# Windowed attention in a four-layer kernel: exponentials divided before they are transposed, global queries' products in column strips, global values spread by a 0/1 matrix

## The chip, the cores and the metric

The kernel runs on one core of one Trainium2 chip. A core has five engines that run side by side, each with its own queue of instructions that it takes strictly in order: TensorE (PE, matrix products and transposes; loading of the stationary operand is shown as PEld), VectorE (DVE), ScalarE (ACT), GpSimd (POOL) and SyncE (SP, which here only issues DMAs). They share the SBUF; TensorE writes its results to eight PSUM banks. The metric is the device time of one execution in microseconds (us).

## The reference

A block of four layers is computed for x of shape 16 x 512 x 256 (16 batches, 512 positions, 256 channels), all in float32. Each layer adds its output to x after a layer norm of x:

```python
x = x + attn_a(layernorm(x))   # stage "a"
x = x + ffn(layernorm(x))      # stage "f"
x = x + attn_b(layernorm(x))   # stage "b"
x = x + ffn(layernorm(x))      # stage "h", the same weights as "f"
```

The change lies in `attn_a` alone. With 16 heads of 16 channels, half a window of 32 and 4 global positions:

```python
q, k, v = proj(Wq, bq), proj(Wk, bk), proj(Wv, bv)
scores = einsum('bhsd,bhtd->bhst', q, k) * 0.25
mask = (abs(i - j) <= 32) | (i < 4) | (j < 4)
attn = softmax(where(mask, scores, -inf))
out = einsum('bhst,bhtd->bhsd', attn, v)
return out @ Wo.T + bo
```

So most queries see a window of 65 keys and the first 4 keys ("global keys"), and the first 4 queries ("global queries") see all 512 keys. `ffn` is a gated product of three 768-wide matrices; `attn_b` is a causal attention over all 512 keys whose denominators come from unrotated queries and keys.

## The kernel before

**What sets the order.** Stages are written as Python generators that yield an `Op` ahead of each piece of work: its engine, an estimated duration, what it needs, which buffers it takes and gives back. `Plan.run` (line 142) keeps all threads of all stages and batches, and again and again puts out the one that can start first by its estimates. On PE, among pieces that can start within 0.05 us, it prefers a lower rank, then one that keeps the same way of lying in the array (`ROWS`, `COLS`: strips of 32; `FULL`), then the thread with the least `progress` (line 137: batch number, plus the stage's `LEAD`, plus the share of the stage's PE time that is done). The order of every engine's queue is therefore fixed when the program is built, and comes from these estimates. Up to four batches are in flight, each in another stage. The planner's estimates (`us=...`, and `LEAD`, `SHARE` in lines 192 and 193) take no part in the computation.

**Stage "a", for one batch** (`window_attention`, line 551). PE makes the keys `kp`, the queries `q` and the values `va` (`values`, line 500). POOL makes masked copies of the 4 global keys and queries, `kg` and `qg`, and `xg`, the first 4 columns of the normalized input repeated 16 times (lines 603 to 614). DMAs on SP copy `va` into two shifted versions `vw`. For each of four tiles `t` of 128 positions, PE makes the scores `sa` of the window (line 663), and then:

- `softmax` (line 674): DVE adds the mask into `sc`, 128 partitions x 16 heads x 132 scores (L693). Each half of eight heads then passes DVE maximum (L706), POOL addition of the negated maximum (L708), ACT exponential (L715) and DVE sum (L717); at the end DVE inverts all 16 sums (L723).
- `turns` (line 763): PE transposes the exponentials in four groups of four 128 x 128 blocks (L772); DVE and ACT take turns at copying them out to `pt` (L777, L779).
- `weights` (line 785): POOL gathers the global keys' exponentials (`pq`, L796) and spreads the inverted sums over 256 channels (`rdca`, L804, shown as the helper's L541). PE transposes `pq` (L809) and both halves of `rdca` (L811) into one PSUM bank; DVE and ACT copy them out to `pgs` (L816, L818).
- The weighted sum: PE multiplies `pt` by `vw` in column strips (L842, four strips of 32 output partitions side by side), and adds the global keys' part from `vg` (L855). `finish` (line 866): DVE multiplies the result by the transposed inverted sums (L872) to give `yt`, and PE projects it (`project_out`, L488).

`global_values` (line 728) makes `vg`, the values of the 4 global keys laid out block-diagonally: PE multiplies `xg` by `wv` (L733, two products, each of which the profile lists as two matmul records, as it does for every float32 product but not for a transpose), and DVE masks it with `g_diag` (L742). `global_queries` (line 883) makes the first 4 queries' outputs over all keys: scores `gq` (L890), maximum, exponential `gp` (64 rows x 512, L905), transposes `tg` (L916), the product with `va` (`og`, L930: four products of 64 x 256, which hold every head's weights against every head's values), the masked and scaled `om` on DVE (L939), and a second product that adds up the rows (`yg`, L945). Its result replaces the first 4 columns of `yt` (L875).

There are two `sc` buffers, and one of most others (the dictionary at line 364). The queries and keys of the next batch can only be made when this batch's last `sa` is done (the slot "a").

Of the kernel before, what the change touches and what calls it, by code (L numbers as in the profile page):

```python
# [191 lines left out]
LEAD = {"a": 0.0, "f": 1.0, "b": 2.0, "h": 3.0}  # L192
# [4 lines left out]
def kernel(  # L197
# [55 lines left out]

    def load_const(ap, shape, name):
        t = const.tile(shape, F32, tag=name, name=name)
        nc.scalar.dma_start(t, ap)
        return t
# [14 lines left out]
    g_sel = cglob[:, D : D + NG]  # L272
# [75 lines left out]
    def values_bias():  # L348
# [3 lines left out]
        for kc in range(NC):  # L352
# [25 lines left out]
            "rdc": 1,  # L378
# [172 lines left out]
    def window_attention(b):  # L551
        me = f"a{b}"

        def go(thread, rank=0):
            plan.start(thread, "a", b, rank)
# [32 lines left out]
        yield from values("a", b, va, wv_sb, 0, "va")  # L588

        def copies():  # L590
# [9 lines left out]
            0, *(f"kp_{me}.{oc}" for oc in range(NC)), *(f"q_{me}.{oc}" for oc in range(NC)), us=2.2  # L600
# [12 lines left out]
        xg = work.tile([P, NC, H, NG], F32, tag="xg", name=f"xg_{b}")  # L613
        nc.gpsimd.tensor_copy(xg, xnt[me][:, :, 0:NG].unsqueeze(2).to_broadcast([P, NC, H, NG]))
# [29 lines left out]
        go(global_values(b, xg))  # L644
# [29 lines left out]
    def softmax(b, t, op, ps, sg):  # L674
# [5 lines left out]
        small = buf(op, "small", [P, 3, H], f"sm_{b}_{t}")  # L680
# [22 lines left out]
        def half(hs, start, name):  # L703
# [10 lines left out]
            op = yield act(1056, op.end, makes=f"sc_{me}.{t}.{name}")  # L714
            nc.scalar.activation(part, part, AF.Exp, scale=SCALE)  # L715
            op = yield dve(0, op.end, us=1.17, makes=f"sum_{me}.{t}.{name}")
            nc.vector.tensor_reduce(small[:, 1, hs], part, AX.X, ALU.add)  # L717

        for n in range(2):
            there = [f"mk_{me}.{t}.{j}" for j in (2 * n, 2 * n + 1)]  # L720
            plan.start(half(slice(n * H // 2, (n + 1) * H // 2), there, n), "a", b, -1)
        op = yield dve(H, f"sum_{me}.{t}.0", f"sum_{me}.{t}.1", makes=f"rden_{me}.{t}")
        nc.vector.reciprocal(  # L723
            small[:, 2, :].rearrange("p (c j two) -> p j c two", c=NC, j=4),
            small[:, 1, :].rearrange("p (j c two) -> p j c two", c=NC, j=4),
        )

    def global_values(b, xg):
        me = f"a{b}"
        op = yield pe(0.9, takes=("u",), gives=(("in_a", 0),))  # L730
        vg_ps = bank(op, [P, S], f"vgp_{b}")
        for kc in range(NC):
            nc.tensor.matmul(  # L733
                vg_ps[: H * NG, :D],
                xg[:, kc],
                wv_sb[:, kc, :],
                start=(kc == 0),
                stop=(kc == NC - 1),
            )
        op = yield dve(D, op.end, f"vgfree_{b}", gives=(("u", op.k["u"]),), makes=f"vg_{me}")  # L740
        vg[b] = work.tile([H * NG, D], F32, tag="vg", name=f"vg_{b}")
        nc.vector.tensor_tensor(vg[b], vg_ps[: H * NG, :D], g_diag, ALU.mult)  # L742
# [4 lines left out]
    def weighted(b):  # L747
# [37 lines left out]
        def weights(t):  # L785

            op = yield pool(
                0, f"sc_{me}.{t}.0", f"sc_{me}.{t}.1", us=0.35, takes=("pq",), makes=f"pq_{me}.{t}"
            )
            sc, small, _, k_small = kept[b, t]  # L790
# [4 lines left out]
            for oc in range(NC):  # L795
# [4 lines left out]
            op = yield pool(  # L800
                0, f"rden_{me}.{t}", us=0.4, takes=("rdc",), gives=(("small", k_small),)
            )
            rdc = work.tile([P, 1, D], F32, tag="rdc", name=f"rdca_{b}_{t}")
            by_channel(small[:, 2:3, :], 1, rdc)  # L804
            op = yield pe(
                0.33, op.end, f"pq_{me}.{t}", takes=("u", "pg"), gives=(("rdc", 0), ("pq", k_pq))
            )
            pg_ps = bank(op, [P, 1 + NC, P], f"pgp_{b}_{t}")
            nc.tensor.transpose(pg_ps[: H * NG, 0, :], pq, ident)  # L809
            for oc in range(NC):  # L810
                nc.tensor.transpose(pg_ps[:, 1 + oc, :], rdc[:, 0, oc * P : (oc + 1) * P], ident)  # L811
            pg = buf(op, "pg", [P, 1 + NC, P], f"pgs_{b}_{t}")
            k_pg, k_u = op.k["pg"], op.k["u"]
            kept[b, t, "pg"] = pg, k_pg
            op = yield dve(P, op.end, makes=f"pg_{me}.{t}")
            nc.vector.tensor_copy(pg[: H * NG, 0, :], pg_ps[: H * NG, 0, :])  # L816
            op = yield act(D, op.end - 0.4, gives=(("u", k_u),), makes=f"db_{me}.{t}")
            nc.scalar.copy(pg[:, 1:, :], pg_ps[:, 1:, :])  # L818

        go(turns())  # L820
        for t in range(NT):
# [31 lines left out]
            pg, k_pg = kept[b, t, "pg"]  # L853
            for c in range(NC):
# [3 lines left out]
                    pg[: H * NG, 0, :],  # L858
# [4 lines left out]
            go(finish(b, t, y_ps, k_u, op.end, pg, k_pg))  # L863


    def finish(b, t, y_ps, k_u, at, pg, k_pg):

        me = f"a{b}"
        op = yield dve(D, at, f"db_{me}.{t}", takes=("yta",), gives=(("u", k_u), ("pg", k_pg)))
        yt = buf(op, "yta", [P, NC, P], f"yt_{b}_{t}")  # L870
        k_yt, there = op.k["yta"], op.end
        nc.vector.tensor_tensor(yt, y_ps, pg[:, 1:, :], ALU.mult)  # L872
# [10 lines left out]
    def global_queries(b, qg):  # L883
# [3 lines left out]
        op = yield pe(1.0, takes=("u", "gs"))  # L887
# [21 lines left out]
        def invert(_):  # L909
            nc.vector.reciprocal(small[:, 3:4], small[:, 2:3])  # L910

        plan.start(one(dve(8, op.end, makes=f"gden_{me}"), invert), "a", b)
        op = yield pe(0.4, op.end, takes=("u",), gives=(("tmp", k_gp),))
        tp = bank(op, [P, NT, R], f"tg_{b}")
        for c in range(NT):
# [5 lines left out]
            1.72,  # L921
            op.end,
            *(f"v_{me}.{t}" for t in range(NT)),
            f"vw_{me}",
            takes=("u",),
            gives=(("pt", op.k["pt"]), ("va", 0)),
        )
        og = bank(op, [P, S], f"og_{b}")
        for c in range(NT):
            nc.tensor.matmul(  # L930
                og[:R, :D],
                pg[:, c, :],
# [453 lines left out]
```

## Time and profile before

| | |
|---|---|
| median of 3 runs | 2706.07 us (2703.79 to 2711.95) |
| the profiled execution, time | 2707.05 us |
| its span, first to last instruction | 2705.3 us |
| PE busy | 2645.4 us, 98% of the span |
| DVE, ACT, POOL busy | 1572.2, 1461.4, 740.3 us (58%, 54%, 27%) |
| mean granted TensorE clock | 0.992 |

How to read it: the profile is of one execution. A group of instructions is shown by its line in the kernel, its engine, and the names of what it writes and reads; matmuls overlap, so the sum of their durations says more than they take, and the distance from one start to the next is the better measure. The timeline lists instructions in order of time, with neighbours of one line merged ("x32").

### The profile page before, as it was taken

The page shows a single profiled execution, that of the slowest core. Times are in us where ns is not written, and L with a number is a line of the kernel's source. Part 1 is how long each engine was busy: PE and PEld are TensorE (multiplying, and loading weights), DVE is VectorE, ACT ScalarE, POOL GpSimd, SP SyncE. Part 2 cuts the span into 40 slices and gives each one's busy share as a digit, 9 for nine tenths or more (in the row PEclk, how much of TensorE's full clock was granted, in tenths as well). Part 3 has the DMA queues.
Part 4 walks back from the last instruction along what each step waited for, and adds up shares of the span by engine and source line. Part 5 has one row for each costly group of instructions (what it writes and reads, how often), then busy time and mean ns, then how long its engine had stood idle before and what let it go on. Part 6 is the DMA issues. An engine that isn't in the chain of part 4 may idle for free.

```text
span 2705.3 us, 52423 instructions
## 1 busy us (share of the span) xinstructions
PE 2645.4 (98%) x21700; PEld 1511.9 (56%) x21700; DVE 1572.2 (58%) x3062; ACT 1461.4 (54%) x3553; POOL 740.3 (27%) x916
## 2 busy tenths in 40 slices
PE   6999999999999999999999999999999999999997
PEld 4655556455565655656466564655656456564444
DVE  7865656466565655746466564565745557464422
ACT  2346564755547455474645647455474654646472
POOL 4323324032241313313133231322313133130201
PEclk8999999999999999999999999999999999999999
DMA  4000010000000000010000100000000000100000
GB/s 134 24 23 1 5 35 1 23 17 23 17 2 23 17 23 17 1 38 2 23 17 6 34 2 23 17 23 17 2 23 17 23 17 1 31 2 8 1 9 8
DMA packets 26574, 49.10 MB, mean 18 GB/s; under 512 B 2336, under 2 KB 21216, under 8 KB 26336
## 3 DMA queue, kind: packets, MB, share of 16 engines
q1 hardware_dynamic: 24976, 44.83, 5.7%
q8 instruction: 170, 2.79, 0.4%
q10 hardware_dynamic: 1360, 0.93, 0.2%
q14 instruction: 68, 0.56, 0.1%
HBM read 13.77 MB, written 8.39 MB: 8 GB/s over the span
## 4 chain that ended last, share of the span: by engine, by line
PE 90%; DVE 6%; issue 3%; ACT 1%; POOL 1%; DMA 0%; ACTq 0%; POOLq 0%; DVEq 0%
PE dn L1102 10%; PE nm L1162 6%; PE psc_gh L534 6%; PE psc_uh L534 6%; PE po_h L488 6%; PE po_f L488 6%; PE psc_uf L534 6%; PE psc_gf L534 6%; PE yb L1222 5%; PE tp L772 4%; PE sa L663 2%; PE ya L842 2%; PE psv_a L512 2%; PE po_a L488 2%; PE psv_b L512 2%
## 5 line engine op out<-in xcount | busy, mean ns | idle before, releaser
L1083 ACT ACTIVATE dn<-dn 128x512 f32<-128x512 f32 x1024 | 598.1, 584 | 136.7 <-PE dn L1102 135.5
L1129 ACT ACTIVATE ptb<-nm 128x512 f32<-128x512 f32 x640 | 329.7, 603 | 278.3 <-PE nm L1162 278.2
L708 POOL TENSOR_TENSOR sc<-sc,sm 128x1056 f32<-128x1056 f32 x128 | 247.4, 1952 | 227.7 <-DVE sm L706 220.7
L1102 PE MATMUL dn<-kt,qb 32*128 32x512 f32 x2048 | 291.6, 635 | 0.0
L1138 POOL TENSOR_SCALAR_AFFINE_SELECT ptb<-ptb 128x512 f32<-128x512 f32 x256 | 157.9, 636 | 446.2 <-ACT ptb L1129 437.9
L715 ACT ACTIVATE sc<-sc 128x1056 f32<-128x1056 f32 x128 | 138.5, 1096 | 137.4 <-POOL sc L708 136.0
L693 DVE TENSOR_TENSOR sc<-sa,mask 128x512 f32<-128x512 f32 x256 | 159.8, 682 | 59.4 <-PE sa L663 59.1
L534 PE MATMUL psc_gh<-xnt_h,wg_sb 128*128 128x512 f32 x384 | 189.2, 615 | 3.2 <-DVE vb L523 3.0
L1083 ACT ACTIVATION_READ_ACCUMULATOR dn<-dn 128x1 f32 x1024 | 191.7, 187 | 0.0
L1162 PE MATMUL nm<-qr,kr 32*128 32x512 f32 (+3 forms) x2048 | 191.0, 461 | 0.4 <-ACT ptb L1129 0.3
L717 DVE TENSOR_REDUCE sm<-sc 128x8 f32<-128x1056 f32 x128 | 157.3, 1242 | 55.2 <-ACT sc L715 55.2
L534 PE MATMUL psc_uh<-xnt_h,wu_sb 128*128 128x512 f32 x384 | 186.9, 609 | 0.0
L534 PE MATMUL psc_gf<-xnt_f,wg_sb 128*128 128x512 f32 x384 | 182.9, 599 | 1.6 <-DVE xnt_f L462 1.6
L534 PE MATMUL psc_uf<-xnt_f,wu_sb 128*128 128x512 f32 x384 | 183.2, 599 | 0.0
L488 PE MATMUL po_h<-wd_sb,ht_h 128*128 128x256 f32 x768 | 181.3, 386 | 0.0
L1102 PEld LDWEIGHTS dn<-kt,qb 32*128 32x128 f32 x2048 | 90.0, 183 | 160.0 <-ACT dn L1083 88.1
L488 PE MATMUL po_f<-wd_sb,ht_f 128*128 128x256 f32 x768 | 179.2, 383 | 0.0
L1222 PE MATMUL yb<-ptb,vb 128*32 128x512 f32 (+3 forms) x2048 | 170.1, 441 | 8.4 <-POOL ptb L1138 8.3
L421 POOL TENSOR_SCALAR rstd_f<-mv_f 128x4 f32<-128x4 f32 x16 | 3.7, 232 | 613.8 <-DVE mv_f L417 613.8
L488 PEld LDWEIGHTS po_h<-wd_sb,ht_h 128*128 128x128 f32 x768 | 141.0, 190 | 45.9 <-issue 13.3
L706 DVE TENSOR_REDUCE sm<-sc 128x8 f32<-128x1056 f32 x128 | 156.3, 1237 | 0.0
L488 PEld LDWEIGHTS po_f<-wd_sb,ht_f 128*128 128x128 f32 x768 | 141.3, 190 | 26.5 <-issue 3.3
(168 smaller groups left out, 4201.3 us busy)
## 6 DMA issues: line engine op xcount, KB each, us to landing
vw<-va SPq DMA_DIRECT2D x32, 576.0 KB, 5.8
x<-in_x_dram SPq DMA_DIRECT2D x16, 512.0 KB, 3.9
out_dram<-x SPq DMA_DIRECT2D x16, 512.0 KB, 2.9
vw<-va SPq DMA_DIRECT2D x32, 144.0 KB, 5.0
raw_wg_sb<-in_w_gate_dram SPq DMA_DIRECT2D x1, 768.0 KB, 8.8
raw_wu_sb<-in_w_up_dram SPq DMA_DIRECT2D x1, 768.0 KB, 10.2
raw_wd_sb<-in_w_down_dram SPq DMA_DIRECT2D x1, 768.0 KB, 10.9
wqkv_sb<-in_wqkv_dram SPq DMA_DIRECT2D x1, 768.0 KB, 11.7
```

The lines of the kernel that those rows point to most:

```text
L488: nc.tensor.matmul(po[:, :D], y_of(c), w_sb[:, c, :], start=(c == 0), stop=(c == n - 1))
L534: nc.tensor.matmul(ps, w_sb[:, kc, lo : lo + P], x_in[:, kc, :], start=(kc == 0), stop=(kc == NC - 1))
L693: nc.vector.tensor_tensor(flat[:, 4 * j : 4 * j + 4, 0:P], ps[j].rearrange("p c two w -> p (c two) w"), mask.unsqueeze(1).to_broadcast([P, ...
L706: nc.vector.tensor_reduce(small[:, 0, hs], part, AX.X, ALU.max, negate=True)
L708: nc.gpsimd.tensor_tensor(part, part, small[:, 0, hs].unsqueeze(2).to_broadcast([P, H // 2, P + NG]), ALU.add,)
L717: nc.vector.tensor_reduce(small[:, 1, hs], part, AX.X, ALU.add)
L1083: nc.scalar.activation(ps[j], ps[j], AF.Exp, scale=SCALE, accum_out=den[:, t, h : h + 1])
L1102: nc.tensor.matmul(ps[j], tiles["qb"][rows, par, oc, t * P : (t + 1) * P], tiles["kt"][rows, oc, :], start=True, stop=True,)
L1129: nc.scalar.activation(pt[:, j, :], ps[j], AF.Exp, scale=SCALE)
L1138: nc.gpsimd.affine_select(out=pt[:, :, at : at + P], in_=pt[:, :, at : at + P], pattern=[[0, 4], [1, P]], compare_op=ALU.is_ge, fill=0.0, ...
L1162: nc.tensor.matmul(ps[j][:, at : at + n], tiles["kr"][rows, oc, c * P : (c + 1) * P], tiles["qr"][rows, par, oc, c * P :], start=True, sto ...
L1222: nc.tensor.matmul(y_ps[rows, c * P :], vb[:, c, 4 * oc + j, par : par + 2, :], pt[:, j, at : at + n], start=len(seen) == 1, stop=len(seen ...
```

## The change

Four things change in stage "a", and the planner's table follows them.

1. The exponentials are divided by their sums in place. Each half of eight heads is followed by a reciprocal of its eight sums on DVE and a POOL product of the half (128 x 1056) with them. The inverted sums are no longer spread and transposed, and `finish` becomes a plain copy, on ACT in place of DVE. Everything that reads `sc` now waits for the POOL product, where it waited for the exponential.
2. The global queries' weights `gp` are divided by their sum on DVE before they are transposed.
3. Their product with the values is made in column strips: 64 products with a stationary operand of 128 x 32 and 4 moving columns, which accumulate straight into the 4 output columns; `om` and the second product `yg` go.
4. The global values are made by one product of a 4 x 64 matrix of zeros and ones, `spread`, with the values of the first 4 positions that are already in `va`; `xg` goes, and the input buffer "in_a" is given back after the last values.

Besides, `LEAD` has other numbers for three stages, `gq` is marked as lying in columns, and some estimates follow.

```diff
-LEAD = {"a": 0.0, "f": 1.0, "b": 2.0, "h": 3.0}
+LEAD = {"a": 0.0, "f": 0.962, "b": 2.002, "h": 2.847}
...
+    spread = const.tile([NG, H, NG], F32, tag="spread", name="spread")
+    nc.gpsimd.tensor_copy(spread, ident[0:NG, 0:NG].unsqueeze(1).to_broadcast([NG, H, NG]))
+    spread = spread.rearrange("p h n -> p (h n)")
...
-        yield from values("a", b, va, wv_sb, 0, "va")
+        yield from values("a", b, va, wv_sb, 0, "va", (("in_a", 0),))
...
-        xg = work.tile([P, NC, H, NG], F32, tag="xg", name=f"xg_{b}")
-        nc.gpsimd.tensor_copy(xg, xnt[me][:, :, 0:NG].unsqueeze(2).to_broadcast([P, NC, H, NG]))
...
-            op = yield act(1056, op.end, makes=f"sc_{me}.{t}.{name}")
+            op = yield act(1056, op.end)
             nc.scalar.activation(part, part, AF.Exp, scale=SCALE)
-            op = yield dve(0, op.end, us=1.17, makes=f"sum_{me}.{t}.{name}")
+            op = yield dve(0, op.end, us=1.17 + 0.15)
             nc.vector.tensor_reduce(small[:, 1, hs], part, AX.X, ALU.add)
+            nc.vector.reciprocal(small[:, 1, hs], small[:, 1, hs])
+            op = yield pool(0, op.end, us=1.9, makes=f"sc_{me}.{t}.{name}")
...
+            nc.gpsimd.tensor_tensor(
+                part,
+                part,
+                small[:, 1, hs].unsqueeze(2).to_broadcast([P, H // 2, P + NG]),
+                ALU.mult,
+            )
...
-        op = yield dve(H, f"sum_{me}.{t}.0", f"sum_{me}.{t}.1", makes=f"rden_{me}.{t}")
-        nc.vector.reciprocal(
...
+        op = yield pe(0.43, f"v_{me}.0", takes=("u",))
+        vg_ps = bank(op, [P, S], f"vgp_{b}")
+        nc.tensor.matmul(
+            vg_ps[: H * NG, :D],
+            spread,
+            va[0:NG, 0, :, 0::2, :],
...
-        for kc in range(NC):
-            nc.tensor.matmul(
-                vg_ps[: H * NG, :D],
-                xg[:, kc],
-                wv_sb[:, kc, :],
...
-            by_channel(small[:, 2:3, :], 1, rdc)
...
-            for oc in range(NC):
-                nc.tensor.transpose(pg_ps[:, 1 + oc, :], rdc[:, 0, oc * P : (oc + 1) * P], ident)
...
-            op = yield act(D, op.end - 0.4, gives=(("u", k_u),), makes=f"db_{me}.{t}")
-            nc.scalar.copy(pg[:, 1:, :], pg_ps[:, 1:, :])
...
-        op = yield dve(D, at, f"db_{me}.{t}", takes=("yta",), gives=(("u", k_u), ("pg", k_pg)))
+        op = yield act(D, at, takes=("yta",), gives=(("u", k_u),))
...
-        nc.vector.tensor_tensor(yt, y_ps, pg[:, 1:, :], ALU.mult)
+        nc.scalar.copy(yt, y_ps)
...
-        op = yield pe(1.0, takes=("u", "gs"))
+        op = yield pe(0.9, takes=("u", "gs"), lying=COLS)
...
+        op = yield dve(0, op.end, us=0.5)
+        nc.vector.reciprocal(small[:, 3:4], small[:, 2:3])
+        nc.vector.tensor_scalar(gp, gp, small[:, 3:4], None, ALU.mult)
...
-                og[:R, :D],
-                pg[:, c, :],
-                va[:, c, :, 0::2, :],
...
+            for oc in range(NC):
+                for par in range(2):
+                    for j in range(4):
+                        at = NG * (8 * oc + 2 * j + par)
+                        nc.tensor.matmul(
+                            og[32 * j : 32 * j + 32, oc, :],
+                            va[:, c, 4 * oc + j, par : par + 2, :],
+                            pg[:, c, at : at + NG],
...
-        om = work.tile([R, D], F32, tag="rdc", name=f"om_{b}")
-        nc.vector.scalar_tensor_tensor(
-            om, og[:R, :D], small[:, 3:4], g_diag, ALU.mult, ALU.mult
...
-                yp[:, oc, :], om[:, oc * P : (oc + 1) * P], g_sel, start=True, stop=True
...
-        nc.vector.tensor_copy(yg, yp)
+        nc.vector.tensor_copy(yg, og)
```

## The prediction

> **What bounds the kernel now.** I read the page's busy times first, then its 40 slices and the chain that ended last. This is the page; the third line is the chain's share by engine.
>
> ```profile
> PE 2645.4 (98%) x21700; PEld 1511.9 (56%) x21700; DVE 1572.2 (58%) x3062; ACT 1461.4 (54%) x3553; POOL 740.3 (27%) x916
> ...
> PE   6999999999999999999999999999999999999997
> ...
> PE 90%; DVE 6%; issue 3%; ACT 1%; POOL 1%; DMA 0%; ACTq 0%; POOLq 0%; DVEq 0%
> ```
>
> PE holds the whole run; only its first and last slices have gaps. Since a busy share can hide a stage with another limit, I asked for busy times by stretch (PE, PEld, DVE, ACT, POOL, then the granted clock):
>
> ```profile
> 34.00:68.00 34.00, 23.86 (x366) 18.15 (x366) 33.18 (x55) 12.64 (x20) 16.98 (x17) 0.75 0.03 8
> 170.00:2400.00 2230.00, 2220.62 (x18436) 1268.13 (x18438) 1319.66 (x2567) 1254.95 (x3071) 620.83 (x759) 1.00 0.06 16
> 2640.00:2706.00 66.00, 51.26 (x282) 27.66 (x280) 17.06 (x35) 17.12 (x33) 8.65 (x14) 0.96 0.03 8
> ```
>
> From 170 to 2400 us PE stands still for only 9.4 of 2230 us, at full clock: there, PE work taken away is time taken away, as long as its queue keeps being fed. The start is another matter: from 34 to 68 us DVE is busy for 33.18 of 34, PE has gaps and runs at 0.75 of its clock, because only batch 0 is there. The end belongs to the later stages, which the change leaves alone. So I sum PE's work first, and then ask where the longer softmax is seen.
>
> **PE's work.** I take distances between starts from PE's timeline (start, duration, line, what; the first two lines are from the start of the run, the rest from later).
>
> ```profile
> 27.28 1.87 PE L626 MATMUL sgp<-kg,q 128*128 128x32 f32 x16
> 29.07 2.17 PE L663 MATMUL sa<-kp,qa 32*64 32x128 f32 x128
> ...
> 113.15 1.94 PE L930 MATMUL og<-va,pgq 128*64 128x256 f32 x8
> 115.02 1.98 PE L534 MATMUL psc_gf<-xnt_f,wg_sb 128*128 128x512 f32 x4
> ...
> 117.38 0.60 PE L945 MATMUL yg<-cglob,om 64*128 64x4 f32 x4
> 117.91 0.65 PE L842 MATMUL ya<-pt,vw 128*32 128x64 f32 x32
> ...
> 1066.29 0.63 PE L842 MATMUL ya<-pt,vw 128*32 128x64 f32 x32
> 1066.74 1.05 PE L1222 MATMUL yb<-ptb,vb 128*32 128x384 f32 x16
> ...
> 1087.87 0.65 PE L842 MATMUL ya<-pt,vw 128*32 128x64 f32 x32
> 1088.46 0.30 PE L809 MATMUL pgp<-ident,pq 128*64 128x128 f32 x1
> 1088.59 0.38 PE L811 MATMUL pgp<-ident,rdca 128*128 128x128 f32 x2
> 1088.81 2.75 PE L488 MATMUL po_f<-wd_sb,ht_f 128*128 128x256 f32 x12
> ```
>
> - The two transposes of the inverted sums: 1088.81 - 1088.59 = 0.22 us a tile, 64 tiles: **-14.1 us**.
> - The second product of the global queries (yg): 117.91 - 117.38 = 0.53 us, 16 batches: **-8.5 us**.
> - Global values: four records become two. A 256-column record takes 1.87 / 8 = 0.234 us in og with its border and 0.216 without (the median distance of its records' starts), so two save 0.43 us, 16 times 6.9. The new one has 4 rows of contraction, and may have to change the array to strips and back. A border costs 0.14 us: the same 32 ya records take 0.45 us ahead of yb, which lies in the same strips, and 0.59 ahead of a transpose. Two of them would cost 0.28 x 16 = 4.5; none, 0. I take 2: **-4.9 us**.
> - og: now 1.87 us a batch. After the change 64 products, 128 records, in 32 rounds of four strips. No row has a 4-column product in a strip. From above, a round costs what ya's does, whose loads are the same 128 x 32 and whose moving columns are 64: 0.45 us / 8 rounds = 56 ns, 1.80 us in all. From below, the loads: sgp, 32 moving columns for a load of 128, shows 16 records in 1.79 us, 112 ns each, so a load of 32 columns is some 28 ns, and if four strips load side by side as ya's do, a round costs 28 ns, 0.90 us in all. I take 32 ns, near the lower end since 4 columns stream 16 times less than ya's 64: 1.02 us, and one border, 1.16 us. Saved 0.71, 16 times: **-11.4 us** (from -13 to +1).
>
> Here a rule of the Trainium skill speaks against the change. "TensorEngine Tiling (Array Packing)", section Instruction Overhead, gives each matmul about 60 cycles however few its columns, and advises not to split where a dimension is small already. At the 2.4 GHz that "TensorE: Matmul & The Clock Gate" states that is 25 ns; charged to each of 128 records, it makes 3.2 us and a border, a loss of 1.47 x 16 = +23.5 us. The ya row weighs against that reading: 32 records in 0.45 us are 14 ns apart, so strips share such an overhead; charged per round it is 25 ns, just under my load bound. I sum with -11.4; by the rule, record by record, the whole would be 34.9 us worse.
>
> gq keeps its products; only its place can move. PE in sum: 14.1 + 8.5 + 4.9 + 11.4 = **-38.9 us**.
>
> **The other engines.** POOL gets 128 products of 128 x 1056, each as the L708 row has it (1.95 us, all of 1946 to 2123 ns): +250; the spreading of sums (L541, 26.3) and xg (6.4) go: +217, to some 957 us, 36% of the span. DVE loses yt (26.8) and om (7.6), and gets 16 scalings of gp, near the sins row's 0.49 us (+7.8), and 128 reciprocals of 8 in place of 64 of 16: between 0.152 (64x1) and 0.244 (128x16), say 0.19, +24 - 16. In sum -18. Against that, POOL's products hold up some DVE instructions:
>
> ```profile
> L549 DVE TENSOR_SCALAR qa<-q,masks x64: 383/504/2470, 21.3 to 2290.3; 128x512 f32<-128x512 f32 x64
> ```
>
> The last of the three is as long as the median and a POOL product together. Mean less median, times count, over this row, its two sisters, L426, L687, L1014 and L1016 comes to about 71 us now; with POOL 29% busier +21. DVE stays where it was. ACT swaps one 128x256 copy (L818, 0.387 us) for another: 0. The new copy waits in ACT's queue for PE's ya, as DVE's product did for 13.6 us in sum; behind it stand stage b's exponentials, which free PSUM banks. ACT has 46% idle; if that cover were gone, PE would lose those 13.6 us. `spread` is one small POOL copy at the start, hidden under the first loads.
>
> **The longer chain.** A tile's transposes wait today for the second exponential; then they will wait for sum 1.24, reciprocal 0.19 and product 1.95: 3.4 us more with nothing in the way, and behind both stand the copies to pt, ya, yt and the projection. In mid-run PE takes other batches' work meanwhile. What it costs if that cover is gone is the second rival below; for in-order queues that meet later than planned I take **+3** (0 to 10). At the start there is no cover. ACT's, PE's and DVE's timelines there:
>
> ```profile
> 45.85 1.09 ACT L715 ACTIVATE sc<-sc 128x1056 f32<-128x1056 f32 x1
> ...
> 46.99 2.40 PE L772 MATMUL tp<-ident,sc 128*128 128x128 f32 x10 [1.29 <-ACT sc L715]
> ...
> 47.89 1.23 DVE L717 TENSOR_REDUCE sm<-sc 128x8 f32<-128x1056 f32 x1
> ```
>
> Batch 0's tile 0 is transposed at 46.99, straight after its second exponential. Its sum ends at 49.1; with reciprocal and product it is 51.3, 4.3 us later. Tile 1's sum (56.08 to 57.3) gives 59.5 against transposes at 56.77: 2.7. Batch 1's queries can't start before the last sa at 61.27, so little else is there; later tiles have it. Together up to 7, and if tile 2 is seen too (sum to 69.5, then 71.6 against 65.45) 13; 0 if the order moves global work into the gap. I take **+6** (0 to 13), for the low clock too. The changed LEAD shifts who goes first, above all in the last 270 us, where PE idles for 26: 0, between -8 and +8, for no row shows it.
>
> **Sum.** -38.9 + 3 + 6 = -29.9 us. The profiled execution's 2707.05 us (span 2705.3 and 1.75 around it) becomes 2677.2; it stands 0.98 over the median, so the median becomes **2676 us**, 1.1% less. Bounds put together (og 0.90 to 1.80, start, mid-run, LEAD) give this case its own range, 2658 to 2694.
>
> **The rivals.** *The small products cost a floor each* (chance 0.10). The rule above speaks for it, ya's spacing against. og is then 3.34 us, and 2676 + 35 = 2711: no change. *PE waits for POOL's product in mid-run, and it gets slower* (0.10). The place is each batch's tiles 2 and 3. In the trace, the median tile is transposed 1.5 us after its last exponential, and in a tenth of them within 0.6: those two go at once, without slack, while tiles 0 and 1 often wait some 20 us for PE. Against it: DVE and POOL have idle time, and PE has three other stages' work at hand; PE stood idle ahead of L772 for L715 only 4.8 us in the whole run, 3.5 of it after 170 us. If PE lost half of the 3.4 us at each of these 32 tiles, 54 us: 2676 + 54 = 2730. It decides from 29.9 / 32 = 0.93 us a tile on. *The chain is free as well* is no case of its own but the lower end of the first: 2667 without both charges.
>
> **How the numbers follow.** The first case has 0.80, nearly all of it under 2698. A change of 0.3% (8 us) is about what can be told from none. Faster 0.79; the same 0.11, from the floor and the first case's edge; slower 0.10. The range, 2656 to 2704, takes in the first case and goes some way to the floor's; outside lie the slow rival, half of the floor's and a little below.
>
> **What would show it.** In the changed kernel's profile the lines of yg, of om and of the rdca transposes are gone, og has 128 records a batch and takes 0.9 to 1.8 us (right) or over 3 (the floor); PE's busy sum is some 40 to 50 us lower; POOL is near 957 us. PE's idle time from 170 to 2400 stays under 20 us, and the first 68 us hold some 6 us more of it. Idle time of PE charged to POOL's product in mid-run would mean the second rival; more than two borders a batch more than now, or a tail 10 us longer, would make the sum wrong elsewhere.

## The result

The changed kernel takes a median of 2686.35 us (2681.33 to 2689.26), against 2706.36 us (2702.38 to 2711.95) for the kernel before on the same chips: a ratio of 0.9925, with an interval of 0.9911 to 0.9940. It is 0.75% faster. The forecast was 2676 us with a range of 2656 to 2704.

The profiled execution took 2689.26 us, its span is 2687.5, so the span is 17.8 us shorter. These lines of its page answer to the three of the kernel before: busy times, PE's 40 slices, and the shares of the chain that ended last.

```profile
PE 2610.2 (97%) x23396; PEld 1494.5 (56%) x23396; DVE 1573.4 (59%) x3062; ACT 1461.5 (54%) x3553; POOL 958.3 (36%) x965
...
PE   5899999999999999999999999999999999999997
...
PE 88%; DVE 9%; POOL 2%; ACT 1%; issue 1%; DMA 0%; ACTq 0%; POOLq 0%; DVEq 0%
```

POOL rose to 958 us as worked out, DVE and ACT did not move, and PE has 35 us less to do. But DVE's share of the chain went from 6% to 9%: some of what PE was spared, it now waits. The busy times by stretch (PE, PEld, DVE, ACT, POOL, then the granted clock) show where:

```profile
34.00:68.00 34.00, 17.66 (x416) 13.36 (x414) 28.20 (x45) 9.74 (x15) 21.22 (x15) 0.70 0.09 22
102.00:136.00 34.00, 27.80 (x273) 14.65 (x280) 24.04 (x47) 10.45 (x16) 15.90 (x12) 0.80 0.01 2
170.00:2400.00 2230.00, 2213.08 (x20308) 1269.83 (x20307) 1344.74 (x2624) 1269.74 (x3098) 825.83 (x821) 1.00 0.06 17
2622.00:2688.00 66.00, 52.57 (x280) 28.59 (x280) 17.08 (x35) 15.70 (x30) 8.04 (x14) 0.94 0.02 9
```

From 34 to 68 us PE has 17.66 us of work where it had 23.86, and there is a second hole from 102 us on, at 0.80 of the clock; the kernel before was busy there for 33.17 of the 34 us, at full clock. In mid-run PE stands idle for 16.9 us where it was 9.4. The last 66 us look as before. The account of the span, with PE's work taken as distances between starts and its idle time counted apart:

| term | forecast | measured |
|---|---|---|
| PE's work, whole run | -38.9 | -35.2 |
| PE idle, 170 to 2400 us (9.4 to 16.9) | +3 | +7.5 |
| PE idle, first 170 us (25.0 to 40.1) | +6 | +15.1 |
| PE idle, from 2400 us on (26.2 to 20.75) | 0 | -5.5 |
| sum | -29.9 | -18.1 (the spans: -17.8) |

PE's part can be seen in mid-run, where everything is full. These are PE's timelines of the kernel before, and then of the changed one, at the scores of the global keys, one batch's after the other's:

```profile
668.04 1.97 PE L626 MATMUL sgp<-kg,q 128*128 128x32 f32 x16
...
995.20 1.97 PE L626 MATMUL sgp<-kg,q 128*128 128x32 f32 x16
```

```profile
679.76 1.94 PE L627 MATMUL sgp<-kg,q 128*128 128x32 f32 x16
...
1002.09 1.94 PE L627 MATMUL sgp<-kg,q 128*128 128x32 f32 x16
```

The line of the batch between them is left out, so the two in a fence are two batches apart: 327.16 us before, 322.33 after, which is 2.42 us a batch. The forecast's sum is 38.9 / 16 = 2.43. So in these two orders the gain per batch is as worked out. (With the old `LEAD`, below, it is not.) Of the 11.8 us by which the sum falls short, 9.1 were lost at the start, 4.5 in mid-run and 3.7 in PE's work; 5.5 came back after 2400 us, where the forecast had nothing and the cause stays open.

**The start.** PE's timeline of the changed kernel, with the idle time ahead of a piece and what ended it in brackets:

```profile
51.44 0.68 PE L909 MATMUL tg<-ident,gp 64*128 64x64 f32 x4 [13.89 <-DVE gp L905]
...
54.40 0.90 PE L778 MATMUL tp<-ident,sc 128*128 128x128 f32 x3
...
107.58 2.30 PE L457 MATMUL lt_f<-ident,xn_f 128*128 128x128 f32 x8 [6.89 <-DVE xn_f L429]
110.50 3.78 PE L537 MATMUL psc_gf<-xnt_f,wg_sb 128*128 128x512 f32 x4 [0.63 <-DVE xnt_f L465]
114.07 3.04 PE L537 MATMUL psc_uf<-xnt_f,wu_sb 128*128 128x512 f32 x4
116.95 1.88 PE L537 MATMUL psc_gf<-xnt_f,wg_sb 128*128 128x512 f32 x4
```

PE's queue holds the transposes of the global queries' weights ahead of batch 0's first tile, and they wait 13.9 us for the new scaling on DVE, which is busy for 28.2 of these 34 us. The tile's transposes start at 54.40; they started at 46.99 before. Their place behind the global queries is the smaller part of this: the tile's two new products on POOL end at 51.11 and 53.20 us, where the forecast had 51.3 for the last. The next stage begins at 107.58, where it began at 92.48. And after the gap PE is slow: its first two groups of four take 3.57 and 2.88 us from start to start, the following ones 1.72, which is another 3.0 us. The clock granted from 103 to 116 us is 0.50, and 1.00 from 117 us on.

### The profile page after: what moved, and what is told of

It reads as the page before. It is cut to its first block, busy times and chain, and to the rows that moved or that the text cites. A ratio compares the mean times of both kernels' runs of the same rounds, so it can differ in the third digit from the quotient of the medians.

```text
span 2687.5 us, 55762 instructions
## 1 busy us (share of the span) xinstructions
PE 2610.2 (97%) x23396; PEld 1494.5 (56%) x23396; DVE 1573.4 (59%) x3062; ACT 1461.5 (54%) x3553; POOL 958.3 (36%) x965
## 4 chain that ended last, share of the span: by engine, by line
PE 88%; DVE 9%; POOL 2%; ACT 1%; issue 1%; DMA 0%; ACTq 0%; POOLq 0%; DVEq 0%
PE dn L1097 10%; PE po_h L491 7%; PE psc_gh L537 7%; PE psc_gf L537 6%; PE psc_uh L537 6%; PE nm L1157 6%; PE psc_uf L537 6%; PE po_f L491 6%; PE yb L1217 6%; PE tp L778 4%; PE sa L664 3%; PE psv_b L515 2%; PE psv_a L515 2%; PE ya L834 2%; PE psc_ka L537 2%; PE po_b L491 2%
## 5 line engine op out<-in xcount | busy, mean ns | idle before, releaser
L709 POOL TENSOR_TENSOR sc<-sc,sm 128x1056 f32<-128x1056 f32 x128 | 247.2, 1952 | 333.1 <-DVE sm L707 326.9
L724 POOL TENSOR_TENSOR sc<-sc,sm 128x1056 f32<-128x1056 f32 x128 | 248.3, 1955 | 101.0 <-DVE sm L719 87.6
```

What stands on the lines that cost most here:

```text
L709: nc.gpsimd.tensor_tensor(part, part, small[:, 0, hs].unsqueeze(2).to_broadcast([P, H // 2, P + NG]), ALU.add,)
L724: nc.gpsimd.tensor_tensor(part, part, small[:, 1, hs].unsqueeze(2).to_broadcast([P, H // 2, P + NG]), ALU.mult,)
```

## The experiments

Every kernel here computes the whole output; only parts of the change are put back, or the order is written differently. Each ratio is to the kernel before. "Start" and "mid-run" are PE's idle time in the first 170 us and from 170 to 2400 us: 25.0 and 9.4 before, 40.1 and 16.9 after.

### Which part gains, which part costs

The first theory was that the gain is a plain sum and the start's longer chain costs the missing 15 us. Without the division (part 1 of the change left out, the rest in place) the kernel should then be about as fast as the changed one; with the division alone, about as fast as before.

The global parts alone:

```diff
+def divided(b):
+    return False
...
+            if not divided(b):
+                op = yield act(1056, op.end, makes=f"sc_{me}.{t}.{name}")
+                nc.scalar.activation(part, part, AF.Exp, scale=SCALE)
+                op = yield dve(0, op.end, us=1.17, makes=f"sum_{me}.{t}.{name}")
+                nc.vector.tensor_reduce(small[:, 1, hs], part, AX.X, ALU.add)
+                return
```

with `rdca`, its transposes and DVE's product for `yt` put back.

> The changed kernel without its first part: the exponentials are not divided in place, the inverted sums are spread, transposed and multiplied in as before; global queries, global values and LEAD as changed. Theory (the division's longer chain at batch 0 costs the start 15 us of idle PE): PE's busy work is 35 - 15 = 20 us under before's, PE's idle time in the first 170 us is back from 40 to some 25 us, the time is about 2685 us, no worse than the changed kernel's 2686. Rival (the start's loss comes from the new order there, with batch 1's normalization ahead of batch 0's masks, which the early return of in_a brings): idle time in the first 170 us stays near 40, and the time is about 2700 us.

Measured: 2699.9 us, 0.9981 (0.9974 to 0.9989). Start 31.3, mid-run 16.4. PE's work is only 18.4 us less than before.

The division alone, with the old global queries and values and the new `LEAD`:

```diff
-        op = yield pe(0.43, f"v_{me}.0", takes=("u",))
+        op = yield pe(0.9, takes=("u",), gives=(("in_a", 0),))
...
+                xg[:, kc],
+                wv_sb[:, kc, :],
```

with "in_a" given back at the global values' product, as in the kernel before.

> The first part alone, with the changed LEAD: division in place, global queries and values as before. Theory: 15 us of transposes saved, 15 us of idle PE at the start gained, about 2705 us, no difference to before. Rival: the start is as before, 25 us idle, and the time is about 2690 us.

Measured: 2813.35 us, 1.0401 (1.0388 to 1.0415). Start 37.2, mid-run 78.3. A part that takes some 15 us of transposes off PE makes the kernel 107 us slower.

The change, with the division left out for batch 0 alone:

```diff
+def divided(b):
+    return b > 0
```

> The changed kernel, with batch 0 alone on the old way (inverted sums transposed and multiplied in); batches 1 to 15 are divided in place. Theory: the start's chain is short again, PE idles some 27 us in place of 40 in the first 170 us, one batch's transposes cost 1 us, and the time is about 2674 us, faster than the changed kernel. Rival (the order at the start, not the division): 40 us idle stay and the time is about 2687 us.

Measured: 2692.76 us, 0.9955 (0.9943 to 0.9967). The start's idle time fell by 7.7 us, to 32.4, but mid-run's rose by 8.2, to 25.1.

The change, with the buffer "in_a" given back as late as before:

```diff
-        yield from values("a", b, va, wv_sb, 0, "va", (("in_a", 0),))
+        yield from values("a", b, va, wv_sb, 0, "va")
...
-        op = yield pe(0.43, f"v_{me}.0", takes=("u",))
+        op = yield pe(0.43, f"v_{me}.0", takes=("u",), gives=(("in_a", 0),))
```

> The changed kernel, with the input buffer in_a given back at the global values' product as before, not after the last values. Theory: no difference, 2686 us within 4. Rival: batch 1's normalization is put after batch 0's masks again, idle time in the first 170 us falls from 40 towards 25 us, and the time is about 2674 us.

Measured: 2716.52 us, 1.0046 (1.0033 to 1.0060). Start 44.0, mid-run 19.7. None of the theories had it slower than before.

What follows: the first theory fell. The parts do not add. Against 2706.36 us, together they gain 20, one alone gains 6, the other alone loses 107. The division does account for 8 of the start's 15 us; the other 7 are there without it too. But what a part costs is not its own work. Each kernel has another order of all five queues, since the planner writes them anew, and something makes some orders bad.

What an order costs is paid again and again, for from about the fifth batch on the timing of each kernel repeats itself, with every batch or every few. Between the fifth batch's scores of the global keys (`sgp`) and the last one's, a batch takes 163.61 us before and 161.15 in the changed kernel. With the division alone it takes 170.67, each single one between 170.65 and 170.77. Over these eleven distances that is 78 us more than before, most of the 107.

### The table of leads

`LEAD` takes no part in the computation, so it can be moved alone: the changed kernel with the old table, the kernel before with the new one, and the division alone with the old one. The expectations name a theory of collisions: POOL's long products hold up some of DVE's instructions, and `LEAD` moves which ones. The next section shows such holds.

```diff
-LEAD = {"a": 0.0, "f": 0.962, "b": 2.002, "h": 2.847}
+LEAD = {"a": 0.0, "f": 1.0, "b": 2.0, "h": 3.0}
```

> The changed kernel with LEAD as before. Prediction's step (LEAD moves the time by 0, between -8 and +8 us): 2678 to 2694 us. Theory of collisions (where POOL's products fall on DVE's two-port instructions depends on how the stages lie against each other, and LEAD sets that): the time moves by more than 8 us, mid-run PE idle time (170 to 2400 us) differs from the changed kernel's 17 us by more than 10, and DVE's instructions that a POOL product holds up are more than in the changed kernel.

Measured: 2708.59 us, 1.0010 (1.0003 to 1.0016). Start 38.9, mid-run 27.6. With the old table all of the rest of the change gains nothing: a batch takes 163.49 us, against 163.61 before. One sign was missed: held-up DVE pieces (counted as below) are fewer than in the changed kernel, 105 against 127, though they lose more, 98 us against 87.

```diff
-LEAD = {"a": 0.0, "f": 1.0, "b": 2.0, "h": 3.0}
+LEAD = {"a": 0.0, "f": 0.962, "b": 2.002, "h": 2.847}
```

> The kernel before with the changed LEAD alone. Prediction's step: within 8 us of 2706. Theory of collisions: the kernel before has half as many POOL products, so it moves less than the changed kernel does; 2695 to 2730 us, with mid-run idle time of PE under 30 us.

Measured: 2707.1 us, 1.0002 (0.9994 to 1.0010). Start 26.7, mid-run 9.5. The same table is worth nothing on the kernel before, and 22 us on the changed one.

> The division alone, with LEAD as before. Theory of collisions: the 2813 us of the division alone came from how the stages lay, and not from the division; here mid-run idle time of PE falls from 78 us to under 40 and the time lies between 2690 and 2760 us. Rival (the prediction's second rival: the chain is too long for PE's cover, whatever the order): mid-run idle stays above 60 us and the time above 2780 us.

Measured: 2770.51 us, 1.0237 (1.0223 to 1.0251). Start 38.7, mid-run 34.9. The time is above the 2760 us that the theory allowed, and below what its rival asked for. So 43 of the 107 us were the table's; the division still loses 64 us without it. The table picks a good order or a bad one. What makes an order bad remained.

### What makes an order bad: is it DVE, held up by POOL?

In the kernel with the division alone and the new `LEAD`, PE's mid-run waits are these (engine and line, what ended the wait: us in total, times, longest):

```profile
PE po_b L489 <- DVE db L1227: 21.1, 11, 1.9
PE tp L779 <- DVE th_f L961: 19.7, 11, 1.8
PE lt_b L455 <- DVE xn_b L427: 12.2, 26, 2.2
```

All for DVE, which is only 61% busy there. The first two come eleven times each: about once in each batch of the repeated order. At one of the longest waits, DVE's, POOL's and PE's timelines of that kernel read:

```profile
1026.33 0.99 DVE L550 TENSOR_SCALAR qa<-q,masks 128x512 f32<-128x512 f32 x2 [0.56 <-ACT q L566]
...
1159.82 3.80 DVE L550 TENSOR_SCALAR qa<-q,masks 128x512 f32<-128x512 f32 x2
1163.54 0.68 DVE L1227 TENSOR_TENSOR db<-yb,db 128x512 f32<-128x512 f32 x1
```

```profile
1158.89 1.95 POOL L724 TENSOR_TENSOR sc<-sc,sm 128x1056 f32<-128x1056 f32 x1 [2.02 <-ACT xnt_b L465]
1160.80 2.53 POOL L440 TENSOR_TENSOR x<-x,bout 128x1024 f32<-128x1024 f32 x1
```

```profile
1161.76 0.60 PE L489 MATMUL po_b<-wout_sb,db 128*128 128x256 f32 x2
1164.27 3.07 PE L489 MATMUL po_b<-wout_sb,db 128*128 128x256 f32 x13 [1.92 <-DVE db L1227]
```

A pair of `qa` pieces takes 0.99 us at 1026.33 and 3.80 us at 1159.82. This second pair begins under POOL's new product (L724, to 1160.84) and ends at 1163.62, 0.3 us after POOL's next long instruction. Its two pieces last 1.31 and 2.57 us; the longer one lies under that next instruction (L440), which the kernel before has too. Behind them in DVE's queue stands `db`, and PE waits 1.92 us for it.

I then took every such DVE piece in the traces (those that read SBUF alone: `qa`, `qb`, `qr`, `xn`, the copy of `sg`, the rotations, `kr`, `gp`) that starts while a POOL product of 128 x 1056 runs. The delay is its duration less the usual one of its line (worked out from the traces):

| kernel | such starts | POOL's remaining time, mean ns | delay, mean ns |
|---|---|---|---|
| before | 15 | 1005 | 847 |
| changed | 23 | 896 | 738 |
| division alone, new `LEAD` | 61 | 1462 | 1260 |

The delay is the remaining time less 0.15 to 0.2 us, with a correlation of 0.99 to 1.00. The starts are not independent: of the 61, 44 are four pieces (`xn_a`, `xn_b`, `qa`, the copy of `sg`) that meet a product again in each of eleven batches. Pieces that read PSUM, and the sums over SBUF (`tensor_reduce`), are not delayed (106 sums in the changed kernel start with 1260 ns of a product left, and last 29 ns longer in the mean). POOL's products wait little in turn: those of L709 in the changed kernel last 1951 ns by the median, 1952 in the mean. The longest, 2133 ns, starts under a `qa` piece with 325 ns to go. The Trainium skill, page "SBUF — State Buffer", section "Who interferes with whom", has this as an exclusive lock on ports shared by the two engines, held for a whole instruction, which a DVE instruction with two SBUF inputs or in a fast two-port mode needs; the traces agree, and show it with `qa`, which has one large SBUF input. The planner knows nothing of it. It puts such pieces where DVE looks free, and everything behind them in DVE's queue is late.

How much of PE's waiting lies behind held pieces can be bounded from the traces. A held piece loses what it lasts beyond the 10th percentile of its line, where that is over 0.2 us. For each mid-run wait of PE for DVE over 0.15 us, I took what held pieces lose in the unbroken run of DVE's work that ends with the awaited piece, up to the wait's length. This covers 54 of 75 us with the division alone and the new `LEAD`, 25 of 30.5 with the old one, and 12 of 14 in the changed kernel; but 11 of 23 in the changed kernel with the old `LEAD`, and 4 of 16 with the global parts alone. So holds can explain most of the waits where the division stands alone, and not everywhere. They are not all the new product's: with the division alone and the new `LEAD` DVE loses 152 us by holds, 74 before; 67 lie under L724, and 23 under L440, where it was 5.

The second theory is therefore: the division adds 128 long POOL products, more DVE pieces run into them and into POOL's other long instructions, DVE is late at places for which the order was not made, and `LEAD` moves who meets whom. Its rival: the chain itself, longer by a sum, a reciprocal and a product, is what PE waits for, or DVE's and POOL's load.

**The product on DVE** takes the second POOL product away, at the price of DVE time:

```diff
-            op = yield dve(0, op.end, us=1.17 + 0.15)
+            op = yield dve(0, op.end, us=1.17 + 0.15 + 1.2, makes=f"sc_{me}.{t}.{name}")
...
-            op = yield pool(0, op.end, us=1.9, makes=f"sc_{me}.{t}.{name}")
...
-            nc.gpsimd.tensor_tensor(
+            nc.vector.tensor_tensor(
```

> The changed kernel with the product of exponentials and inverted sums on DVE, straight behind the sum, in place of POOL (128 x about 1.2 us more on DVE, 248 us less on POOL). Theory of collisions: DVE instructions held up by POOL get fewer than before the change, tiles are ready 0.8 us or more sooner, mid-run idle time of PE is under 17 us and the time 2670 to 2684 us. Rival (DVE, 59% busy, becomes the late engine at 64%): mid-run idle time of PE over 30 us and the time over 2695 us.

Measured: 2756.9 us, 1.0187 (1.0173 to 1.0200). Start 39.4, mid-run 55.7. DVE is busy for 1433 of mid-run's 2230 us (1345 in the changed kernel), and PE's longest mid-run waits in this kernel are all for it:

```profile
PE psc_qb L537 <- DVE xnt_b L465: 12.0, 8, 1.8
PE yb L1216 <- DVE th_f L960: 9.4, 4, 2.4
PE lt_h L457 <- DVE xn_h L429: 6.2, 10, 0.9
PE psc_uf L537 <- DVE pt L782: 5.3, 4, 1.7
```

Here the rival's forecast came true, with 88 us more work on DVE in mid-run. But DVE still loses 89 us by holds (87 in the changed kernel), since POOL's other long instructions stay. The run says that POOL is the better place for the product; it does not test the holds by themselves.

**Telling the planner.** A sharper test leaves every instruction as it is and changes the order alone: DVE pieces that need the shared ports are planned to start no earlier than the end of a long POOL instruction, less 0.15 us.

```diff
+        self.big = 0.0
...
+                if op.port:
+                    start = max(start, self.big)
...
+            if engine == "pool" and us >= 0.6:
+                self.big = start + us - 0.15
...
-                op = yield dve(0, op.end - 0.17 if par else op.end, us=0.4)
+                op = yield dve(0, op.end - 0.17 if par else op.end, us=0.4, port=True)
```

and `port=True` likewise on `xn`, `qb`, `qr`, the copy of `sg`, the rotations and, in the changed kernel, `gp`. First with the division alone, old `LEAD`:

> The division alone with LEAD as before (2770.5 us), and a planner that knows of the hold: a DVE piece that reads two SBUF operands or runs on two ports is not planned to start before the last long POOL piece (0.6 us or more) ends. The engines' instructions are the same, only their order changes. Theory of collisions (the unplanned holds make DVE late, and PE waits for it): mid-run idle time of PE falls from 35 us to under 22, time lost by held-up DVE instructions falls, and the time is 2700 to 2745 us. Rival (the order is bad for another reason, such as the later release of in_a or the longer chain itself): within 15 us of 2770.

Measured: 2719.32 us, 1.0046 (1.0033 to 1.0058): 51 us less than without the rule. Start 33.8 in place of 38.7, mid-run 20.4 in place of 34.9. Of PE's waits for `xn_h`, the first line is the kernel without the rule, the second the one with it:

```profile
PE lt_h L455 <- DVE xn_h L427: 16.9, 20, 1.0
```

```profile
PE lt_h L460 <- DVE xn_h L432: 0.9, 1, 0.9
```

One expectation missed: the time that DVE loses by holds (as defined above) did not fall: 105.0 us without the rule, 105.6 with it. The holds are as long as before; what fell is PE's waiting for DVE in mid-run, from 30.5 to 7.7 us. That is not the whole gain either: of the 51 us, 20 are idle time of PE, and 31 lie in its busy time (2667.2 to 2636.1 us) with the same instructions. About 9 of these are time at half the clock (PE busy for 46 us at a granted 0.50, then 28); the rest is not explained.

Then the changed kernel with the rule and the old `LEAD`:

> The changed kernel with LEAD as before (2708.6 us) and the same planner that knows of the hold. Theory of collisions: the 22 us that the changed LEAD was worth come back without it, at least in half: 2680 to 2698 us. Rival: within 8 us of 2708.

Measured: 2691.79 us, 0.9942 (0.9928 to 0.9955): 17 us less than with the old `LEAD` alone. The rule gives back most of what the new `LEAD` was worth. Start 32.3, mid-run 25.5: mid-run's idle time, where the theory has its sign, is only 2 us less than the 27.6 without the rule.

Any new rule shuffles the whole order, so the gain might be luck. The control puts the same rule, with the division alone, on the wrong DVE pieces: the two of the gated product and the additions to `x`, which read PSUM and are not held.

```diff
-            op = yield dve(S, op.end, gives=(("u", k),))
+            op = yield dve(S, op.end, gives=(("u", k),), port=True)
...
-            op = yield dve(S, at, f"up_{me}.{f}", makes=f"ht_{me}.{f}")
+            op = yield dve(S, at, f"up_{me}.{f}", makes=f"ht_{me}.{f}", port=True)
```

> A control for the run with the planner that knows of the hold: the division alone, LEAD as before (2770.5 us), the same rule in the planner, but put on DVE pieces that POOL doesn't hold up, since they read PSUM (both pieces of the gated product, and the addition of a projection to x). It makes another order, with no knowledge in it. Theory of collisions: no gain like the 51 us of the true rule; over 2745 us. Rival (any other order would have been better than that unlucky one): under 2730 us.

Measured: 2758.32 us, 1.0188 (1.0174 to 1.0202): 12 us less than without a rule, against 51 with it on the right pieces. Start 38.1, mid-run 27.3. That is as the theory expected, but it doesn't prove it. One control is one other order, and the two tables of `LEAD`, which know nothing of holds, are 43 us apart on this same part. With the control, too, PE's waits for DVE fall from 30.5 us to 14.5, while DVE loses more by holds, 130 us; and of the 39 us between control and rule 30 lie in PE's busy time (2666.3 and 2636.1 us). So the rule gives a good order twice; that it does so by knowing which pieces are held is likely, and not shown.

### The three together

The changed kernel with the rule, estimates set to the durations in the traces, and a `LEAD` chosen for the order that ends first by the planner's own estimates:

```diff
-LEAD = {"a": 0.0, "f": 0.962, "b": 2.002, "h": 2.847}
+LEAD = {"a": 0.0, "f": 0.908, "b": 1.881, "h": 3.0}
...
-            op = yield dve(0, *start, us=1.17)
+            op = yield dve(0, *start, us=1.24)
...
-            op = yield pool(0, op.end, us=1.9)
+            op = yield pool(0, op.end, us=1.96)
```

> The changed kernel with the planner that knows of the hold, estimates of the softmax's pieces as the profile measures them (1.24, 1.96, 1.09 us), and LEAD f 0.908, b 1.881, h 3.0, chosen for the shortest plan. Theory of collisions: PE's mid-run idle time under 12 us, 2660 to 2682 us, faster than the changed kernel. Rival (what the planner doesn't know decides): 2686 us or more.

Measured: 2683.02 us, 0.9911 (0.9897 to 0.9924). Start 27.5, mid-run 18.8, short of what was expected for mid-run and just past the upper edge of the time. It beats the kernel before; against the changed kernel (0.9911 to 0.9940) the intervals overlap, so a gain over it isn't shown. Its start has lost most of the 15 us, but its work on PE is only 30.2 us below before's, where the changed kernel has 35.2.

## Why the prediction was right, and where it was not

The time fell inside the range, 10 us above the forecast, and the likeliest case is the one that happened: PE's work shrank and the time followed. By steps:

- **PE's work: right.** -38.9 forecast, -35.2 measured. The rdca transposes gave 15.3 (14.1), yg 8.6 (8.5), the global values 7.0 (4.9), og 10.5 (11.4). These make 41.4; elsewhere PE takes 6.2 us more. The slow clock alone would do that: PE is busy for 44 us at a granted 0.50, against 27 before, some 8.5 us by half the difference (3 in the first 170 us, the rest later).
- **og in strips: right, and the Trainium skill's rule of 60 cycles a matmul ("TensorEngine Tiling (Array Packing)", section Instruction Overhead) refuted as read record by record.** The changed kernel's timeline shows all 128 records in 1.12 us, with `ya` following in the same strips:

```profile
130.48 1.25 PE L929 MATMUL og<-pgq,va 128*32 128x4 f32 x128
131.60 0.68 PE L834 MATMUL ya<-pt,vw 128*32 128x64 f32 x32
```

  That is 35 ns for a round of four strips (32 was taken). A batch costs 1.21 us with its border, where 1.16 was forecast and the record-by-record reading gave 3.34. The first rival has no place left.
- **POOL, DVE and ACT in sum: right.** POOL 958.3 (957). DVE 1573.4 against 1572.2, and ACT 1461.5 against 1461.4, both unchanged as forecast; the reciprocals of 8 take 203 ns (190).
- **The start: failed on size.** +6 (0 to 13) forecast, +15.1 measured. About 8 us are the division's (left out for batch 0, the idle time falls from 40.1 to 32.4). About 7 are not: the kernel with the global parts alone also has 31.3, 6 above before. The forecast gave the reordering at the start either nothing or a gain; it cost as much as the longer chain, and the low clock after the gap 3 us, which lie in PE's work.
- **The mid-run chain: within its bounds.** +3 (0 to 10) forecast, +7.5 measured. PE waits for POOL's product for 0.6 us in the whole run:

```profile
PE psc_gh L537 <- DVE xnt_h L465: 7.3, 13, 0.8
...
PE tp L778 <- POOL sc L724: 0.6, 2, 0.3
```

  The second rival's mechanism is absent here. What PE does wait for is DVE. It is not absent from every order: in the control above PE waits for that product for 8.7 us in mid-run, in 12 waits.
- **LEAD: failed.** "0, between -8 and +8, for no row shows it" was right for the kernel before (2707.1 us) and wrong for the changed one, where the table is worth 22 us. It was priced as a shift of who goes first, felt above all in the tail. But of the 22 us, 10.7 lie in mid-run's idle time (27.6 to 16.9) and 9.9 in PE's work from start to start (25.3 below before's, and 35.2), which holds short waits too.
- **"Against that, POOL's products hold up some DVE instructions ... DVE stays where it was": failed as a cost of nothing.** The holds were seen, and their +21 us of DVE were left hidden in its idle time. In the changed kernel DVE's lost time rose from 74 to 87 us and little of it is seen. But with the division alone the kernel is 64 us slower, 107 with the new `LEAD`, and most of PE's mid-run waits for DVE there lie behind held pieces. The trace shows where a held piece costs: where the order has put something for PE right behind it.
- **The bounds: the upper one is added up wrongly.** The lower bounds (og, start, mid-run, LEAD) add up to 2657 us, about the 2658 given. The upper ones, added in the same way, reach 2710, where 2694 was given.
- **The tail: +0 forecast, -5.5 measured.** This helped the total; its cause stays open.

The saving in PE's work was worked out rightly. That the time showed it was in part luck: two terms that were both set to about nothing, the new `LEAD` and what the rest of the change does to the order, nearly cancelled. With the old `LEAD` the same change measures 2708.6 us, above the range.

Giving "in_a" back late costs 30 us, though DVE is held less there than in the changed kernel (71 pieces, 63 us, against 127 and 87). Half of it can be read from the clock: PE is busy for 74 us at a granted 0.50, against 44, which makes some 15 us. Another 8 us are idle time. Why this order meets the low clock more often is open, for even the same wait does not always bring it. PE's timeline of that kernel:

```profile
1490.13 1.12 PE L1097 MATMUL dn<-kt,qb 32*128 32x512 f32 x2 [0.78 <-DVE ht_h L967]
1491.18 1.13 PE L515 MATMUL psv_b<-wqkv_sb,xnt_b 128*128 128x256 f32 x4
...
1652.18 1.12 PE L1097 MATMUL dn<-kt,qb 32*128 32x512 f32 x2 [0.78 <-DVE ht_h L967]
1653.23 2.05 PE L515 MATMUL psv_b<-wqkv_sb,xnt_b 128*128 128x256 f32 x4
```

The same wait of 0.78 us comes once a batch, ten times from 842 us on. After the first five, of which 1490.13 is the last, the clock stays whole; after the other five it is granted at 0.50 for 3.4 us, from 1653.3 us on after the one at 1652.18, and a batch takes 1.7 us longer.

Left open: which of the other parts' reorderings costs the 7 us at the start; how much of the holds' effect another shuffle of the order might have given, beyond the one control; whether the late return of "in_a", which the kernels with the division alone have too, is part of their loss; and where the busy time of PE that differs between orders of the same instructions goes, beyond the clock.

## What to carry to other kernels

Where the queues' order is fixed ahead by estimates, an edit's price is its own work plus what the new order does, and the second can be the larger: measure the edit with the planner's table as it was and with the new one, and each part alone, before believing a sum. Where batches repeat one order, a wait that looks small in the trace is paid once a batch. A new long POOL instruction is not free because POOL is idle: list the DVE instructions that read only SBUF, see how their longest durations end with POOL's, and try whether keeping them out of its way, or letting the planner know of it, gives a better order. Small products in column strips were cheap here, where four strips run side by side: price a round of four, not a record.

## What the runs showed of the hardware

- A DVE instruction of the kinds listed above that starts under one of POOL's 128 x 1056 products ends about its own duration after it, less 0.15 to 0.2 us: `qa` takes 0.486 us by its median and up to 2.170. This line of the changed kernel's trace has its shortest, median and longest (ns):

```profile
L552 DVE TENSOR_SCALAR qa<-q,masks x64: 435/486/2170, 23.1 to 2277.6; 128x512 f32<-128x512 f32 x64
```

- Not every DVE piece that reads SBUF is held: in the changed kernel 106 sums over 1056 SBUF elements lose 29 ns in the mean under such a product, and 16 copies of `sg` within SBUF lose 540 ns, with 673 ns of it left.
- A product of 4 moving columns costs 9 ns when four strips take turns (1.12 us for 128 records).
- After an idle stretch of 6.9 us PE ran slowly for its next few us: four 128x512 records took 3.57 us, then 2.88, then 1.72, with a granted clock of 0.50 from 103 to 116 us and 1.00 from 117 us on. In one kernel a wait of 0.78 us, once a batch, was followed by 3.4 us at 0.50 in five batches, and by the whole clock in the five before.
